# Six blocks' x and W1 products moved to the first steps of a graph layer kernel on one core

## The chip, the core and the metric

The kernel runs on one core of a Trainium2 chip. Its engines work side by side, each through its own list of instructions in program order: TensorE (PE in the profile; its weight loads are PEld), VectorE (DVE), ScalarE (ACT), GpSimd (POOL) and SyncE (SP), which here issues most DMAs. Matrix products land in PSUM banks, everything else lies in SBUF. The metric is the device time of one execution in microseconds (us); lower is better.

## The reference

One layer of a graph network with 12,500 nodes of 128 numbers and 412,500 edges of 48 numbers, sorted by destination:

```python
h   = relu(layernorm(x))                                  # 12500 x 128
agg = segment_sum(edge_attr_48, dst, num_segments=12500)  # 12500 x 48
u   = graph_globals[0]                                    # the same 64 numbers for every node
hid = relu(concat([h, agg, u]) @ W1 + b1)                 # 12500 x 256
out = x + hid @ W2 + b2                                   # 12500 x 128
```

All numbers are float32. Nearly all bytes that are read are the edges.

## The kernel before

**Edges.** They are taken in 58 steps (the last one smaller) of 8 chunks of 896 edges. A step's edges come in four loads (`load`, line 279) of 336 KB. VectorE compares destinations with a row of 0 to 31 (`onehot`, line 290); TensorE multiplies the one-hot matrices with the edges (`aggregate`, line 314) into a bank "ps"; ScalarE copies the bank to SBUF (`keep_sums`, line 335); VectorE makes a second one-hot matrix that places the chunks' windows (`place_columns`, line 352); two steps later TensorE multiplies with it (`place`, line 358) and VectorE adds the result to the running sums `aggT` (`add`, line 366). `aggT` lies as one column per node and has 112 rows; it is cleared in 16 parts of 797 columns, each part two steps before it is needed (`zero`, line 581).

**Nodes.** They are taken in 26 blocks: block 0 has 212 nodes (2 rows of 106), the others 512 (4 rows of 128), the last two 256 each. For a block, x is loaded (`load_x`), VectorE takes mean and variance (`stats`), ScalarE a root (`root`), VectorE makes scale and shift (`factors`), ScalarE normalises (`normal`, tile xn), TensorE transposes (`turn`, bank "pt"), ScalarE copies that to SBUF (`keep`, tile hT), TensorE multiplies with W1's rows for x (`first_h`, two halves, banks "ph") and later adds W1's rows for the sums (`first_a`) in the same bank, ScalarE adds the bias and cuts at zero (`relu`, tile hid), TensorE multiplies with W2 (`second`, bank "po"), VectorE adds x + b2 (`result`; GpSimd has made that sum in `plus_b2`), and GpSimd's queue stores it. A block's `first_a` can run only when the sums of all its nodes are there; its `first_h` needs only x.

**Banks.** "ph" has two buffers, "pt" and "po" have one each. A bank is written again only when whoever reads it is done.

**Order.** The schedule is written out by hand: the order in which the program issues instructions is the order of each engine. Each step s has two half-steps, 2s and 2s+1; `at(k, f, ...)` puts a function into half-step k, behind what was put there before. In a step come: `place` of two steps earlier, the work of half-step 2s, `add`, the work of half-step 2s+1, the step's `aggregate`, `keep_sums`, `place_columns`, and `onehot` of two steps later. The four loads of step s+3 stand between these. The pieces `turn`, `first_h`, `first_a`, `second` are put by a small planner (`piece`, line 643): each half-step has room for 1.25 us of such work (plus up to 0.5 left over, or what is lacking, from the half-step before), a piece goes to the first half-step from its due time on, and not before the piece put last, where the room is at least half its cost; costs are 0.16 r for `turn`, 0.22 r for each `first_h`, 0.27 r for `first_a`, 0.9 for each half of `second`, with r rows in the block. In steps with little such work, some pairs of edge products are put together as one of twice the width, which has fewer instructions and takes longer.

**Loads.** SyncE issues them in order. At most five counted loads are under way (`few`, line 272): each waits until the one five before it has landed. From step 1 on each also waits for the last TensorE instruction put in front of it.

**Other work near the start.** Destinations come in parts: part 0 (steps 0 to 3) and part 1 (16 steps) early. `shift_dst` and `own_and_ref` run on VectorE, `spread_dst` turns them on TensorE and copies on ScalarE, `middles` uses TensorE and then VectorE (part 0 in bank "po"). `check_dst` (line 261) is a check of the destinations on ScalarE, at half-steps 10 and 12 for parts 0 and 1. `bias_of_globals` (line 510) uses "po" as well. `spare` (line 593) is a product whose result is not used.

Of the kernel before, what the change touches and what calls it, by code (L numbers as in the profile page):

```python
# [8 lines left out]
F32 = mybir.dt.float32  # L9
# [13 lines left out]
def kernel(  # L23
# [75 lines left out]

    parts = [(0, 4 * CS)]  # L100
# [7 lines left out]
    aggT = const.tile([HI + DE, N + WG], F32)  # L108
# [32 lines left out]
    with fast:  # L141
# [224 lines left out]
        def add(s):  # L366
            _, v = nc.values_load_multi_w_load_instructions(
                at_i[0:1, s:s + 1], engines=[DVE], min_val=low(s), max_val=high(s),
                skip_runtime_bounds_check_because="clamped to these on the chip")
            to = aggT[:, ds(v[0], WG)]  # L370
            nc.vector.tensor_tensor(to, to, banks_p.pop(s)[:HI + DE, :WG], OP.add)  # L371

        def load_x(j):
            a, m, r = blocks[j]
            xt = xp.tile([P, 4, D], F32, name="xt")
            xv = xt.rearrange("p r d -> p (r d)")[:, :r * D]
            for p0, p1 in by_rows(m):
                now = nc.sync.dma_start(xv[p0:p1], rows_of(x, a + p0 * r, p1 - p0, r))
            if j > 1:
                few(now)  # L380
            xs[j] = xt
# [26 lines left out]
        def plus_b2(j):  # L408
            a, m, r = blocks[j]
            xb = mp.tile([P, 4, D], F32, name="xb", bufs=4)  # L410
            nc.gpsimd.tensor_tensor(xb[:m, :r], xs[j][:m, :r], b2_sb[:m, None, :].to_broadcast([m, r, D]), OP.add)  # L411
            xbs[j] = xb
# [9 lines left out]
        def turn(j):  # L422
            a, m, r = blocks[j]
            pt = ps_t.tile([P, 512], F32, name="pt")
            for q in range(r):
                transposed(pt[:, q * m:(q + 1) * m], ht[j][:m, q], ident[:m, :m])
            ht[j] = pt
# [20 lines left out]
        def first_h(j, h):  # L448
            n, small, ph = bank(j, h)
            product(ph, w1h[:, h * P:(h + 1) * P], ht[j][:, :n], start=(h == 0 or not small),  # L450
                             stop=False, skip_group_check=True)
            hids[j, h] = ph

        def first_a(j):
            a, m, r = blocks[j]
            n = m * r
            for q in range(0, n, 256):
                w = min(256, n - q)  # L460
                for h in range(NH):
                    c = BEFORE + a + q
                    k = slice(0, DE) if bank_is_shared(j) else slice(HI * h, HI * h + DE)
                    product(hids[j, h][:, q:q + w], w1a[k, h * P:(h + 1) * P], aggT[k, c:c + w],
                                     start=False, stop=True, skip_group_check=True)
# [92 lines left out]
        with tc.manual_schedule():  # L558
# [14 lines left out]
            ZN = 16  # L573
            zw = -(-aggT.shape[1] // ZN)

# [5 lines left out]
            def zero(i):  # L581
                nc.gpsimd.memset(aggT[:, i * zw:min((i + 1) * zw, aggT.shape[1])], 0.0)
# [72 lines left out]

            def behind(name, j):
                return where[name, j] // 2 * 2 + 2

            def turned(j):
                k = 8 + 3 * j if j < 2 else 2 * placed(ready[j]) - 2  # L660
                piece("turn", j, k, 0.16 * blocks[j][2], (turn, (j,)), (keep, (j,)))

            def hidden_x(j):
                us = 0.22 * blocks[j][2]
# [19 lines left out]
            for j in range(NBL):  # L684
                k = where["turn", j]
                if j > 1:
                    at(k - 17, load_x, j)
                near = j < 2
                at(k - (6 if near else 8), stats, j)
                at(k - (4 if near else 6), root, j)  # L690
# [6 lines left out]
            taken = {where["turn", j] for j in range(NBL)}  # L697
# [255 lines left out]
```

## Time and profile before

| | |
|---|---|
| median of 3 runs | 313.0 us (307.3 to 314.23) |
| the profiled execution | 310.81 us, its span 309.1 us |
| PE busy | 291.4 us (94%) |
| DVE busy | 231.8 us (75%) |
| ACT busy | 164.1 us (53%) |
| POOL busy | 78.5 us (25%) |
| moved by DMA | 95.15 MB, mean 308 GB/s |

The span runs from the first to the last instruction of the program; the profiled execution's own time is a little longer than its span. Busy time is the union of an engine's instructions, averaged over stages that differ, so the table alone does not say what sets the end.

### The profile page before, as it was taken

How to read it: one execution, taken by the hardware profiler on the slowest of the kernel's cores; microseconds unless marked ns; L12 is line 12 of the kernel's file. 1: busy time of each engine (PE TensorE's matmuls, PEld its weight loads, DVE VectorE, ACT ScalarE, POOL GpSimd, SP SyncE). 2: the span in 40 equal slices, each digit the busy share in tenths (PEclk: the TensorE clock that was granted, in tenths of full speed). 3: DMA queues.
4: the chain of work that ended last, by engine and by line, in shares of the span. 5: the costliest groups of instructions: out<-in, count | busy, mean ns of one | idle time of the engine just before them, and what ended most of it. 6: DMA issues, size and time to landing. Idle time of an engine off the chain costs nothing. (4 is left out here: it accounts for less than half of the span.)

```text
span 309.1 us, 14799 instructions
## 1 busy us (share of the span) xinstructions
PE 291.4 (94%) x6397; PEld 227.5 (74%) x6398; DVE 231.8 (75%) x530; ACT 164.1 (53%) x426; POOL 78.5 (25%) x87
## 2 busy tenths in 40 slices
PE   7888999999999999989999999999999899999982
PEld 3577767767877877866877887876887777786772
DVE  6867958987695967759976598779984899797221
ACT  2223696465564764645454487655452884665320
POOL 8221041032120544222134204123303033223000
PEclk9997999999999999999999999999999999999999
DMA  7999999999999999999999999999999999998102
GB/s 231 313 322 316 338 338 336 343 361 296 336 344 333 365 349 331 312 333 287 319 354 326 363 335 333 346 348 322 315 367 312 289 354 321 375 357 279 39 0 75
DMA packets 69717, 95.15 MB, mean 308 GB/s; under 512 B 5018, under 2 KB 64611, under 8 KB 69647
## 3 DMA queue, kind: packets, MB, share of 16 engines
q1 hardware_dynamic: 67439, 87.53, 85.3%
q0 software_dynamic: 2208, 6.63, 5.6%
q8 instruction: 51, 0.84, 1.1%
q14 instruction: 19, 0.16, 0.1%
HBM read 87.74 MB, written 6.40 MB: 305 GB/s over the span
## 5 line engine op out<-in xcount | busy, mean ns | idle before, releaser
L178 PE MATMUL ps<-e,oh 128*32 128x48 f32 (+1 forms) x5288 | 117.6, 218 | 7.2 <-issue 4.6
L178 PEld LDWEIGHTS ps<-e,oh 128*32 128x32 f32 (+1 forms) x5288 | 100.7, 116 | 31.4 <-issue 10.2
L294 DVE TENSOR_TENSOR oh<-iota,rel 128x1792 f32<-128x1792 f32 (+1 forms) x60 | 116.0, 1936 | 0.0
L340 ACT COPY sums<-ps 128x192 f32<-128x192 f32 (+1 forms) x165 | 43.1, 262 | 97.5 <-PE ps L178 94.9
L497 POOL DMA_DIRECT2D out_dram<-ot x25 | 14.0, 560 | 207.9 <-DVE ot L489 156.1
L371 DVE TENSOR_TENSOR aggT<-aggT,pp 112x246 f32 x58 | 23.7, 409 | 39.6 <-PE pp L178 30.3
L411 POOL TENSOR_TENSOR xb<-xt,b_sb 128x512 f32<-128x512 f32 (+2 forms) x26 | 46.5, 1792 | 15.3 <-DMA xt<-in_x_dram 9.8
L178 PE MATMUL po<-w,hid 128*128 128x128 f32 (+1 forms) x384 | 47.7, 276 | 1.3 <-ACTq L815 1.3
L178 PE MATMUL ph<-hT,w1h 128*128 128x512 f32 (+2 forms) x100 | 47.5, 578 | 0.6 <-ACT hT L432 0.6
L178 PEld LDWEIGHTS po<-w,hid 128*128 128x128 f32 (+1 forms) x384 | 44.9, 191 | 2.2 <-ACTq L815 1.4
L475 ACT ACTIVATE hid<-ph,bias 128x512 f32<-128x512 f32 (+2 forms) x49 | 30.4, 670 | 24.5 <-PE ph L178 23.3
L418 ACT ACTIVATE xn<-xt,sh,sc 128x128 f32<-128x128 f32 (+1 forms) x98 | 40.5, 483 | 0.5
L178 PE MATMUL pp<-place,sums 128*112 128x128 f32 x232 | 39.7, 295 | 0.0
L178 PEld LDWEIGHTS pp<-place,sums 128*112 128x112 f32 x232 | 29.2, 178 | 7.6 <-issue 1.5
L354 DVE TENSOR_TENSOR place<-iota,pos 128x256 f32<-128x256 f32 x58 | 34.3, 593 | 0.0
L178 PE MATMUL ph<-aggT,w1a 48*128 48x256 f32 (+1 forms) x192 | 28.3, 400 | 0.0
L432 ACT COPY hT<-pt 128x512 f32<-128x512 f32 (+2 forms) x26 | 26.7, 1026 | 3.1 <-PE pt L182 3.1
L489 DVE TENSOR_TENSOR ot<-po,xb 128x512 f32<-128x512 f32 (+2 forms) x25 | 16.6, 665 | 13.5 <-PE po L178 12.2
L178 PEld LDWEIGHTS ph<-aggT,w1a 48*128 48x128 f32 x192 | 17.3, 186 | 10.9 <-issue 7.8
L388 DVE BATCH_NORM_STATS2 st<-xt 128x6 f32<-128x128 f32 (+1 forms) x98 | 21.3, 279 | 1.8 <-DMA xt<-in_x_dram 1.8
L178 PEld LDWEIGHTS ph<-hT,w1h 128*128 128x128 f32 x100 | 16.2, 191 | 6.4 <-issue 3.3
L182 PE MATMUL pt<-ident,xn 128*128 128x128 f32 (+1 forms) x98 | 15.9, 282 | 0.0
(120 smaller groups left out, 139.7 us busy)
## 6 DMA issues: line engine op xcount, KB each, us to landing
e<-in_edge_attr_dram SPq DMA_DIRECT2D x230, 336.0 KB, 5.1
xt<-in_x_dram SPq DMA_DIRECT2D x23, 256.0 KB, 4.8
out_dram<-ot POOLq DMA_DIRECT2D x23, 256.0 KB, 5.5
di<-in_dst_dram SPq DMA_DIRECT2D x3, 448.0 KB, 6.9
xt<-in_x_dram SPq DMA_DIRECT2D x2, 128.0 KB, 4.2
out_dram<-ot SPq DMA_DIRECT2D x2, 128.0 KB, 2.6
di<-in_dst_dram SPq DMA_DIRECT2D x1, 154.0 KB
w1h<-in_L_gnn_W_dram POOLq DMA_DIRECT2D x1, 128.0 KB, 5.6
```

Source lines behind the costliest of these rows:

```text
L178: last[:] = [nc.tensor.matmul(*a, **k).ins.name]
L182: last[:] = [nc.tensor.transpose(*a, **k).ins.name]
L294: nc.vector.tensor_tensor(to, iota[:, None, :W].to_broadcast([P, n, W]), r[:, :, None].to_broadcast([P, n, W]), OP.is_equal)
L340: nc.scalar.copy(to[k, h], ps[k, h, None, o:o + DE].to_broadcast([k.stop - k.start, h.stop - h.start, 2, DE]))
L354: nc.vector.tensor_tensor(po, iota[:, None, :WP].to_broadcast([P, 2, WP]), pos[:, s, :, None].to_broadcast([P, 2, WP]), OP.is_equal)
L371: nc.vector.tensor_tensor(to, to, banks_p.pop(s)[:HI + DE, :WG], OP.add)
L388: nc.vector.bn_stats(st[:m, q, :], xs[j][:m, q, :])
L411: nc.gpsimd.tensor_tensor(xb[:m, :r], xs[j][:m, :r], b2_sb[:m, None, :].to_broadcast([m, r, D]), OP.add)
L418: nc.scalar.activation(xn[:m, q], xs[j][:m, q], AF.Relu, bias=shift[j][:m, q:q + 1], scale=scale[j][:m, q:q + 1])
L432: nc.scalar.copy(hT[:, :m * r].rearrange("d (p r) -> d r p", r=r), ht[j][:, :m * r].rearrange("d (r p) -> d r p", r=r))
L475: nc.scalar.activation(to, ph, AF.Relu, bias=bias[:, h:h + 1])
L489: nc.vector.tensor_tensor(ot[:m, :r], pos_o[j][:m, :r], xbs[j][:m, :r], OP.add)
```

## The change

Six blocks (`FIRST`, in the order 1, 2, 0, 3, 4, 5) get their x and their x W1 products early. x of these blocks and the products lie in columns of `aggT` that are cleared and used only later; `aggT` gets all 128 rows for this, while sums still use 112. The products are copied out of the bank on ScalarE (`keep_h`) and added back on VectorE (`add_h`) when the block's sums are there. The transposes of these blocks use bank "po". x of block 1 is loaded ahead of all edges, the others between the edge loads of steps 1 to 4; part 1 of the destinations is loaded between step 1's edge loads. All weights but W1's rows for x are loaded behind step 1's work. Two spare products go, and some of the early work on destinations moves by a half-step or a step.

```diff
+    FIRST = (1, 2, 0, 3, 4, 5)
+    ZN = 16
+    zw = -(-(N + WG) // ZN)
...
-    aggT = const.tile([HI + DE, N + WG], F32)
+    aggT = const.tile([P, N + WG], F32)
+    kept_x, kept_h = {}, {}
+    c0 = 4 * zw
+    for j in sorted(FIRST):
+        n = blocks[j][1] * blocks[j][2]
+        kept_x[j] = aggT[:, c0:c0 + blocks[j][2] * D].rearrange("p (r d) -> p r d", d=D)
+        c0 += blocks[j][2] * D
+        kept_h[j] = aggT[:, c0:c0 + NH * n].rearrange("p (h n) -> p h n", h=NH)
+        c0 += NH * n
...
-            xt = xp.tile([P, 4, D], F32, name="xt")
+            xt = kept_x[j] if j in FIRST else xp.tile([P, 4, D], F32, name="xt")
...
-            if j > 1:
+            if j != FIRST[0]:
                 few(now)
...
-            xb = mp.tile([P, 4, D], F32, name="xb", bufs=4)
+            xb = xs[j] if j in FIRST else mp.tile([P, 4, D], F32, name="xb", bufs=4)
...
-            pt = ps_t.tile([P, 512], F32, name="pt")
+            pt = ps_o.tile([P, 512], F32, name="po") if j in FIRST else ps_t.tile([P, 512], F32, name="pt")
...
-                             stop=False, skip_group_check=True)
+                             stop=j in FIRST, skip_group_check=True)
...
+        def keep_h(j, h):
+            if bank_is_shared(j):
+                n = blocks[j][1] * blocks[j][2]
+                nc.scalar.copy(kept_h[j], banks[j].rearrange("p (h n) -> p h n", h=NH)[:, :, :n])
+            else:
+                nc.scalar.copy(kept_h[j][:, h], hids[j, h])
+
+        def add_h(j):
+            if bank_is_shared(j):
+                n = blocks[j][1] * blocks[j][2]
+                to = banks[j].rearrange("p (h n) -> p h n", h=NH)[:, :, :n]
+                nc.vector.tensor_tensor(to, to, kept_h[j], OP.add)
+            else:
+                for h in range(NH):
+                    nc.vector.tensor_tensor(hids[j, h], hids[j, h], kept_h[j][:, h], OP.add)
...
         def load_weights():
             nc.gpsimd.dma_start(w1h, W1[0:D])
-            nc.gpsimd.dma_start(w1a[0:DE], W1[D:D + DE])
+
+        def load_weights_of_sums():
+            now = nc.gpsimd.dma_start(w1a[0:DE], W1[D:D + DE])
+            tc.add_manual_dep(now.ins, last[0], LANDED, reason="edges first")
...
+            load_x(FIRST[0])
             load_step(0)
+            load(1, 0)
+            load(1, 1)
             load_dst(1)
-            load_x(0)
-            load_step(1)
+            load(1, 2)
+            load(1, 3)
+            load_x(FIRST[1])
             load_step(2)
-            load_x(1)
+            load_x(FIRST[2])
+            load_x(FIRST[3])
             for s in range(3, AHEAD):
                 load_step(s)
+            load_x(FIRST[4])
...
+            for i, j in enumerate(FIRST):
+                r = blocks[j][2]
+                if i == len(FIRST) - 1:
+                    at(2, load_x, j)
+                at(2 * i, stats, j)
+                at(2 * i + 1, root, j)
+                at(2 * i + 1, factors, j)
+            for i, j in enumerate(FIRST):
+                at(2 * i + 2, normal, j)
+            for i, j in enumerate(FIRST):
+                r = blocks[j][2]
+                for k, us in ((2 * i + 3, 0.16 * r), (2 * i + 4, 0.44 * r)):
+                    room[k] = room.get(k, SHARE) - us
+                    work[k] = work.get(k, 0.0) + us
+                at(2 * i + 3, turn, j)
+                at(2 * i + 3, keep, j)
+                for h in range(NH):
+                    at(2 * i + 4, first_h, j, h)
+                    if h or not bank_is_shared(j):
+                        at(2 * i + 4, keep_h, j, h)
+                at(2 * i + 5, plus_b2, j)
...
-                piece("a", j, 2 * placed(ready[j]) + (4 if j == 0 else 2), 0.27 * r, (first_a, (j,)), (relu, (j,)))
+                piece("a", j, 2 * placed(ready[j]) + (4 if j == 0 else 2), 0.27 * r, (first_a, (j,)), *([(add_h, (j,))] if j in FIRST else []), (relu, (j,)))
...
-            at(0, shift_dst, 1)
-            at(2, spread_dst, 1, 0)
-            at(2, spread_dst, 1, 1)
+            at(2, shift_dst, 1)
+            at(4, spread_dst, 1, 0)
+            at(4, spread_dst, 1, 1)
             at(2, middles, 0)
-            at(4, own_and_ref, 1)
-            at(6, middles, 1)
+            at(3, load_weights_of_sums)
+            at(5, own_and_ref, 1)
+            at(7, middles, 1)
             at(10, check_dst, 0)
             at(12, check_dst, 1)
-            for k in (1, 3):
-                at(k, spare)
```

For the six blocks the planner places only `first_a` (with `add_h`) and `second`; their `turn`, `first_h` and the work around them stand at the half-steps written above, and `first_a` starts the bank anew.

More of the change, by code (lines that the diff above doesn't have):

```diff
@@ L107 @@
     relt = const.tile([P, T], F32)
-    aggT = const.tile([HI + DE, N + WG], F32)
+    aggT = const.tile([P, N + WG], F32)
[7 more added lines that the diff above has]
+        c0 += NH * n
+    assert c0 <= N + WG
     at_i = const.tile([1, NSP], I32)
@@ L369, in add @@
                 skip_runtime_bounds_check_because="clamped to these on the chip")
-            to = aggT[:, ds(v[0], WG)]
+            to = aggT[:HI + DE, ds(v[0], WG)]
             nc.vector.tensor_tensor(to, to, banks_p.pop(s)[:HI + DE, :WG], OP.add)
@@ L458, in first_a @@
             n = m * r
+            if j in FIRST:
+                for h in range(NH):
+                    _, small, hids[j, h] = bank(j, h)
             for q in range(0, n, 256):
@@ L461, in first_a @@
                 for h in range(NH):
+                    begin = j in FIRST and q == 0 and (h == 0 or not small)
                     c = BEFORE + a + q
@@ L464, in first_a @@
                     product(hids[j, h][:, q:q + w], w1a[k, h * P:(h + 1) * P], aggT[k, c:c + w],
-                                     start=False, stop=True, skip_group_check=True)
+                                     start=begin, stop=True, skip_group_check=True)
         def relu(j):
@@ L572 @@
                            allow_small_or_imprecise_dtypes=True)
-            ZN = 16
-            zw = -(-aggT.shape[1] // ZN)
             def clear_tail():
@@ L581, in zero @@
             def zero(i):
-                nc.gpsimd.memset(aggT[:, i * zw:min((i + 1) * zw, aggT.shape[1])], 0.0)
+                nc.gpsimd.memset(aggT[:HI + DE, i * zw:min((i + 1) * zw, aggT.shape[1])], 0.0)
             zero(0)
@@ L653 @@
             piece.last = 0
+            for i, j in enumerate(FIRST):
[14 more added lines that the diff above has]
+                at(2 * i + 3, keep, j)
+                for h in range(NH):
+                    at(2 * i + 4, first_h, j, h)
+                    if h or not bank_is_shared(j):
+                        at(2 * i + 4, keep_h, j, h)
+                at(2 * i + 5, plus_b2, j)
             def behind(name, j):
@@ L659, in turned @@
             def turned(j):
-                k = 8 + 3 * j if j < 2 else 2 * placed(ready[j]) - 2
+                if j in FIRST:
+                    return
+                k = 2 * placed(ready[j]) - 2
                 piece("turn", j, k, 0.16 * blocks[j][2], (turn, (j,)), (keep, (j,)))
             def hidden_x(j):
+                if j in FIRST:
+                    return
                 us = 0.22 * blocks[j][2]
@@ L684 @@
             for j in range(NBL):
+                if j in FIRST:
+                    continue
                 k = where["turn", j]
[L686 to L690, printed above, removed]
+                at(k - 17, load_x, j)
+                at(k - 8, stats, j)
+                at(k - 6, root, j)
                 at(k - 4, factors, j)
@@ L694 @@
             at(where["a", 0] - 2, bias_of_globals)
-            taken = {where["turn", j] for j in range(NBL)}
+            taken = {where["turn", j] for j in range(NBL) if j not in FIRST}
             def apart(k, f, *a):
```

## The prediction

> **What bounds the kernel now.** I read the page's slices first, then the windows, then the timelines of TensorE (PE), ScalarE (ACT), VectorE (DVE) and SyncE (SP) over the first 100 us, where the change lies.
>
> ```profile
> DMA  7999999999999999999999999999999999998102
> ...
> 20.00:40.00 20.00, 17.10 (x333) 14.54 (x332) 16.46 (x51) 10.11 (x30) 3.24 (x3) 0.91 1.00 330
> 40.00:60.00 20.00, 20.00 (x455) 15.29 (x456) 15.51 (x35) 14.56 (x38) 5.70 (x6) 1.00 1.02 338
> ...
> 290.00:300.00 10.00, 10.00 (x225) 8.29 (x224) 2.31 (x6) 2.71 (x7) 0.00 (x0) 1.00 0.06 23
> ```
>
> The first row gives the DMA engines' busy share in 40 slices, the others PE, PEld, DVE, ACT and POOL (each with its count), then PE's clock, the DMA share and GB/s. Two resources are full at once: the DMA engines from the second slice until the edges are in, and PE from 40 us to the end, where it works on alone (DMA 0.06). Both limits have to be followed.
>
> ```profile
> 17.00 1.37 PE L178 MATMUL ps<-e,oh 128*64 128x96 f32 x26 [0.54 <-DMA e<-in_edge_attr_dram]
> ...
> 25.72 2.50 PE L178 MATMUL ps<-e,oh 128*64 128x96 f32 x26 [0.58 <-DMA e<-in_edge_attr_dram]
> ...
> 39.89 1.98 PE L178 MATMUL ph<-hT,w1h 128*128 128x512 f32 x4 [0.61 <-ACT hT L432]
> ...
> 159.70 2.49 PE L178 MATMUL ps<-e,oh 128*32 128x48 f32 x84
> ```
>
> The columns are start, duration, engine, line, operation, tiles, count and the wait before it. In steps 1 to 5 PE waits for edges (the first two rows); from then on the loads run a little ahead and PE is late by its own work, in program order. The third row is the one I weigh most: the product of x and W1 of block 1 waits 0.61 us for ScalarE's copy hT, because ScalarE, also in order, had to finish something else first. The last row (step 30) took 2.49 us where an equal group takes 2.11 (45.80 below): a short wait of about 0.4 us, the only place after step 5 where I find the loads still setting the pace. So time that PE loses before step 30 is time lost at the end, but for 0.4 us; time that PE gains before step 30 is given back to the loads there.
>
> **The change, part by part.** It moves, for six blocks, the turning of x and the products with W1 from steps 4 to 15 into steps 1 to 7, adds a copy out of the sums' bank on ScalarE (keep_h) and an addition on VectorE (add_h), and removes two spare products. PE's prices are start-to-start differences of these rows.
>
> ```profile
> 45.80 2.11 PE L178 MATMUL ps<-e,oh 128*32 128x48 f32 x84
> 47.83 0.69 PE L178 MATMUL pp<-place,sums 128*112 128x128 f32 x4
> 48.36 1.95 PE L178 MATMUL po<-w,hid 128*128 128x128 f32 x16
> 50.15 1.02 PE L178 MATMUL ph<-hT,w1h 128*128 128x512 f32 x2
> 51.10 1.87 PE L178 MATMUL ps<-e,oh 128*32 128x48 f32 x96
> 52.90 0.69 PE L178 MATMUL pp<-place,sums 128*112 128x128 f32 x4
> ...
> 54.38 1.14 PE L178 MATMUL ph<-aggT,w1a 48*128 48x256 f32 x8
> 55.45 0.66 PE L182 MATMUL pt<-ident,xn 128*128 128x128 f32 x4
> 56.03 1.87 PE L178 MATMUL ps<-e,oh 128*32 128x48 f32 x96
> ...
> 92.51 0.69 PE L178 MATMUL pp<-place,sums 128*112 128x128 f32 x4
> ```
>
> A step's edges: 2.03 us (84 records) to 1.80 (96). Placing: 0.53. Second layer of a block: 1.79. One product of x and W1: 0.95, so 1.9 for both halves. Product of the sums: 1.07. Turning: 0.58. Step 7 ends at 47.83 and step 16 at 92.51.
>
> ```profile
> 12.23 0.73 PE L182 MATMUL pt<-ident,df 128*128 128x128 f32 x4 [1.37 <-DVE df L198]
> ...
> 13.26 0.38 PE L178 MATMUL po<-own,same_c 32*128 32x8 f32 x2
> ...
> 13.92 1.13 PE L178 MATMUL ph<-iota,ones 128*128 128x512 f32 x2
> ...
> 29.14 0.36 PE L182 MATMUL pt<-ident,xn 106*128 106x106 f32 x2
> 29.43 0.60 PE L178 MATMUL po<-u,w1u 64*128 64x1 f32 x4
> ...
> 33.44 0.88 PE L178 MATMUL ph<-hT,w1h 128*128 128x212 f32 x4
> 34.25 0.98 PE L178 MATMUL ph<-aggT,w1a 48*128 48x212 f32 x4
> ...
> 35.75 2.03 PE L178 MATMUL ps<-e,oh 128*32 128x48 f32 x88
> ```
>
> Turning destinations: 1.03; middles: 0.66; a spare pair: 1.13. The small block 0: turning 0.29, products with W1 0.81, with the sums 0.9. Bias: 0.6.
>
> ```profile
> 35.93 0.93 ACT L258 ACTIVATE sc<-df 32x896 f32<-32x896 f32 x1
> ...
> 38.79 1.05 ACT L432 COPY hT<-pt 128x512 f32<-128x512 f32 x1
> 39.63 0.87 ACT L340 COPY sums<-ps 128x192 f32<-128x192 f32 x3
> 40.53 1.65 ACT L418 ACTIVATE xn<-xt,sh,sc 128x128 f32<-128x128 f32 x4
> 42.08 0.94 ACT L258 ACTIVATE sc<-df 128x896 f32<-128x896 f32 x1
> ...
> 44.98 0.28 ACT L397 ACTIVATE sc<-mv,eps 128x4 f32<-128x4 f32 x1
> ...
> 13.00 0.60 ACT L252 COPY rel<-pt 128x512 f32<-128x512 f32 x1 [1.26 <-PE pt L182]
> ```
>
> On ScalarE hT costs 1.05, keeping the sums 0.87, normalising 1.55, a root 0.3. check_dst(0), from 35.93 to 38.79, costs 2.86 and check_dst(1), from 42.08 to 44.98, costs 2.90: these are what hT stood behind in the row above. keep_h is not in this trace; a copy of the same size out of a bank took 0.60 (13.00) and hT, which also reorders, 1.05. I take 0.55, nearest to the plain copy; with 1.05 each a block would pay 1.0 more on ScalarE.
>
> *Step 1.* Its turning of block 1 writes the bank "po" (one buffer), which middles(0) used just before; VectorE reads that bank only after it has done, in order, the statistics of block 2 and shift_dst.
>
> ```profile
> 11.21 0.15 DVE L196 CAST first<-di 128x1 f32<-128x1 int32 x1 [1.14 <-DMA di<-in_dst_dram]
> ...
> 12.00 2.02 DVE L294 TENSOR_TENSOR oh<-iota,rel 128x1792 f32<-128x1792 f32 x1
> ...
> 21.27 0.87 DVE L388 BATCH_NORM_STATS2 st<-xt 128x6 f32<-128x128 f32 x4 [0.24 <-DMA xt<-in_x_dram]
> ...
> 22.34 0.53 DVE L354 TENSOR_TENSOR place<-iota,pos 128x256 f32<-128x256 f32 x1
> ```
>
> Block 2's x is loaded behind step 1's last edges, which landed at 17.00; the new order puts block 1's x ahead of them and the small loads of weights behind, so I leave 17.0 for it. Statistics 1.07 and shift 0.79 give 18.9, some short reads 19.3, turning 19.9, edges 22.0. Before, step 1 ended at 18.4: 3.6 late. The spare products that filled this wait are gone.
>
> *Steps 2 and 3.* 0.53 + 1.9 + 1.03 + 0.58 + 1.9 = 5.9 and 0.53 + 1.9 + 0.29 + 0.66 + 1.9 = 5.3. End 33.2.
>
> *Step 4.* Turning waits for xn, ready 0.87 + 1.55 = 2.4 into the step; bias_of_globals uses po too and waits for hT (root 0.3, then 1.05) until 4.4. Then 0.6 + 2.03: 7.0 us, 2.5 of them waits.
>
> *Step 5.* 0.53 + 1.9 + 0.58 + 0.9 + 1.8 = 5.7, with 0.3 of waits 6.0. But ScalarE does sums 0.87, xn 1.55, two keep_h 1.1, check_dst(0) 2.86, root 0.3, hT 1.05, so hT of block 4 is ready 7.8 into the step.
>
> *Step 6.* PE starts at 6.0 of that clock, and block 4's products wait from 6.5 to 7.8. ScalarE then does block 0's relu (0.7), sums and xn, until 10.9: turning of block 5 ends at 11.5. Then keep_h twice and check_dst(1), 4.0, and hT, 1.05: 15.9. The second layer of block 0 stands next on PE, needs po, and waits for that copy: 4.4 us. With 0.9 for it and 1.7 for the edges the step ends at 18.5, that is 12.5 us long.
>
> *Step 7.* 0.53 + 1.9 + 0.6 of wait for a bank + 1.07 + 1.75 = 5.9.
>
> Sum: 22.0 + 5.9 + 5.3 + 7.0 + 6.0 + 12.5 + 5.9 = 64.6 against 47.8: 16.8 late. (The planner's room at even half-steps is 1.25 - 1.76, below zero there, which is what puts block 0's second layer at half-step 13, next to that turning.)
>
> *Steps 8 to 16* have lost the moved work: nine times 0.53 + 2.03, four products of sums 4.3, four second layers 7.2, one turning, 0.9 of destinations: 36.1 against 92.5 - 47.8 = 44.7. That gives 8.6 back, and 8.2 remain. From step 17 the plan is the old one by its totals.
>
> *Loads.* They are issued three steps ahead, tied to PE's pace.
>
> ```profile
> 43.23 0.34 SPq L378 DMA_DIRECT2D xt<-in_x_dram  x1
> ```
>
> This load (block 5, issued in step 5) could have gone when PE had done step 5's small work (35.75), and went 7.5 us later, being held by the loads before it. So a PE up to 7.5 us late stops no load; one 16.8 late stops them for about 9.3 us, which DMA engines at 1.00 can't make up. The two limits give nearly the same loss, 8.2 and 9.3.
>
> ```profile
> 26.00:29.00 3.00, 3.00 (x30) 2.78 (x29) 2.22 (x15) 0.70 (x3) 1.27 (x1) 0.50 0.88 276
> ```
>
> *Clock.* Behind the short waits of step 3 PE was granted 0.50, and the group at 25.72 took 2.50 instead of 1.37, 1.1 more. The changed kernel has two longer holes (some 6 us in step 1, 4.4 in step 6): 2.2 us. The Trainium skill, "TensorE: Matmul & The Clock Gate", in "Why this matters for your kernels", says that a hole of about 3 us takes the clock to half; here a clock of 0.50 followed waits of which the longest was 0.58, so the trace is less forgiving than the page. By its window of about 3.4 us at half speed the two holes would cost an estimated 3.4.
>
> *Hidden.* add_h goes to VectorE, 15.51 of 20 us busy:
>
> ```profile
> L489 DVE TENSOR_TENSOR ot<-po,xb 128x512 f32<-128x512 f32 (+2 forms) x25 | 16.6, 665 | 13.5 <-PE po L178 12.2
> ```
>
> An addition from a bank costs 0.67, so 1.3 a block, about what the moved statistics free; uncovered on PE, five and a half blocks would be 7 us. The weights that POOL now issues behind step 1's work are first needed in step 4, after 33 us, and would cost only what they landed later than that; the moved x loads keep SP's order and bytes, apart from blocks 4 and 5 coming some steps earlier; the additions of b2 run on POOL, wanted only by the results.
>
> **Sum:** 8.2 to 9.3, plus 2.2 for the clock, less 0.4 at step 30: +10 to +11.1. The profiled execution took 310.8 (span 309.1 and 1.7 around it), 2.2 below the median of 313.0. I forecast 310.8 + 10.7 = 321.5.
>
> **Rivals.** (1) *No change that shows*: if ScalarE's copies don't hold PE (hT ready in time, po free), steps 4 to 7 lose 2.5 + 0.3 + 7.0 + 0.6 = 10.4 less; 6.4 late at step 7 is less than the 8.6 given back and less than the 7.5 that stops loads. Then the loads decide at step 30: 310.4, and with half the waits about 314. For it: DMA at 1.00 throughout. Against: the wait at 39.89. (2) *Faster*: the early holes of PE (2.9 us in 20:40, 1.1 of slow clock, 2.3 of spare products) are filled and the loads turn out able to go faster with PE ahead: 310.8 - 6.3 = 304.5. Against: a DMA share of 1.00 leaves no such speed. (3) *Heavier*: keep_h costs 1.05, which adds 1.0 on ScalarE in front of hT in each of steps 2 to 6: 321.5 + 5 = 326.5, and to 330 if the loads, stopped as much longer, are then the limit. For it: ScalarE is the engine that holds PE; against: the plain copy's 0.60.
>
> **How the numbers follow.** Forecast (316 to 326) 0.62; no change 0.20; faster 0.08; heavier 0.10. Leaving out the faster case and the far end of the heavier one gives 310 to 328. Over 2% is about 6.3 us, roughly what a measurement of this kernel tells from no change: slower 0.68, same 0.24, faster 0.08.
>
> **What would show it.** On PE a second-layer product po<-w,hid of block 0 in step 6 that waits some 4 us for ACT hT; first products of block 4 that wait for hT; a turning in step 1 that waits for DVE; a DMA share below 0.9 somewhere between 40 and 65 us; step 7 ending near 65. It is wrong if ScalarE is idle there, if the DMA share stays at 1.00, or if PE catches up before step 30 by more than 8.6 us.

## The result and the profile after

The changed kernel takes 327.38 us in the median (327.18 to 330.79), against 310.83 us for the kernel before on the same chip: a ratio of 1.0618, 95% interval 1.0495 to 1.0740. Executions of one kernel differ by a few per cent, and all ratios here compare the faster ones alone, so they aren't the quotients of the medians. The changed kernel's profiled execution took 327.18 us with a span of 325.4, against 310.81 and 309.1: 16.3 us more.

The slices of the page of the changed kernel, in the order PE, clock, DMA:

```profile
PE   7489695699999999999899999999999999999992
...
PEclk9969989599999999999999999999999999999998
DMA  7999965289999999999999999999999999999302
```

Where DMA had a row of nines there is now a hole in slices 6 to 8 (40 to 65 us); PE has holes in slices 2, 5, 7 and 8, and its clock dips three times. The page gives 95.15 MB for both kernels: nothing more is moved, but for a while less per us. The same in windows of 10 us (columns as in the prediction: PE, PEld, DVE, ACT, POOL, clock, DMA share, GB/s):

```profile
40.00:50.00 10.00, 9.67 (x209) 7.54 (x209) 3.91 (x12) 6.13 (x17) 1.26 (x1) 0.84 0.71 216
50.00:60.00 10.00, 3.97 (x12) 1.80 (x12) 5.71 (x8) 9.17 (x24) 0.00 (x0) 0.84 0.39 116
60.00:70.00 10.00, 9.95 (x237) 7.25 (x237) 2.94 (x6) 3.32 (x8) 3.05 (x4) 0.81 0.57 161
70.00:80.00 10.00, 10.00 (x218) 9.00 (x218) 8.53 (x10) 3.46 (x11) 0.60 (x1) 1.00 0.89 276
80.00:90.00 10.00, 9.55 (x256) 8.22 (x258) 8.35 (x18) 2.85 (x8) 1.33 (x2) 1.00 1.01 338
```

From 40 to 80 us the DMA engines lose (0.29 + 0.61 + 0.43 + 0.11) x 10 = 14.4 us of their time; after that they are full again and can't win it back. That is nearly the whole loss of 16.3; TensorE's own lateness, further down, is as large. Between 50 and 60 ScalarE is busy for 9.17 us and TensorE for 3.97.

Who stops the loads stands in SyncE's waits of the changed kernel between 35 and 75 us (what it waited for: us in total, times, longest):

```profile
SPq L142 <- PE po L193: 9.1, 2, 7.7
SPq L142 <- PE ps L193: 6.7, 4, 3.0
SPq L142 <- PE po L197: 5.1, 3, 3.1
...
SPq L142 <- DMA e<-in_edge_attr_dram: 2.4, 5, 0.5
```

The edge loads wait for TensorE, to whose pace they are tied, and hardly for earlier loads. TensorE's own timeline in the changed kernel shows what it waited for:

```profile
17.88 1.08 PE L197 MATMUL po<-ident,xn 128*128 128x128 f32 x4 [6.30 <-DVE dev L254]
18.90 3.79 PE L193 MATMUL ps<-e,oh 128*32 128x48 f32 x84
...
39.45 0.70 PE L193 MATMUL po<-u,w1u 64*128 64x1 f32 x4 [2.74 <-ACT hT L447]
40.09 3.54 PE L193 MATMUL ps<-e,oh 128*32 128x48 f32 x84
...
51.31 1.98 PE L193 MATMUL ph<-hT,w1h 128*128 128x512 f32 x4 [1.21 <-ACT hT L447]
...
59.42 2.04 PE L193 MATMUL po<-w,hid 128*106 128x128 f32 x8 [4.62 <-ACT hT L447]
61.40 2.64 PE L193 MATMUL ps<-e,oh 128*32 128x48 f32 x108
...
69.75 0.69 PE L193 MATMUL pp<-place,sums 128*112 128x128 f32 x4
```

Three long waits: the turning in step 1 for VectorE (6.30), the bias in step 4 (2.74) and block 0's second layer in step 6 (4.62), both for ScalarE's hT. Behind each, the edge products are slow: 3.79 and 3.54 us for the 84 records that took 2.11 at 45.80 in the kernel before, and 2.64 for 108 records that took 1.63 in the version with bank "pt" below. Step 7 ends at 69.8 instead of 47.8, 22.0 late.

ScalarE in step 6, on its own timeline of the changed kernel, is what the prediction described:

```profile
54.45 1.07 ACT L475 COPY aggT<-ph 128x512 f32<-128x512 f32 x2
55.41 0.96 ACT L273 ACTIVATE sc<-df 128x896 f32<-128x896 f32 x1
...
58.34 1.03 ACT L447 COPY hT<-po 128x512 f32<-128x512 f32 x1
```

Two copies keep_h (0.53 each), then the check of the destinations from 55.41 to 58.34, and only then the hT for which "po" and so the second layer wait.

### The profile page after: what moved, and what is told of

Same layout as the page of the kernel before. It is cut to its first block, busy times and chain, and to the rows that moved or that the text cites. A ratio compares the mean times of both kernels' runs of the same rounds, so it can differ in the third digit from the quotient of the medians.

```text
span 325.4 us, 14757 instructions
## 1 busy us (share of the span) xinstructions
PE 296.6 (91%) x6373; PEld 232.0 (71%) x6374; DVE 238.6 (73%) x541; ACT 169.4 (52%) x437; POOL 75.8 (23%) x87
## 2 busy tenths in 40 slices
DMA packets 69717, 95.15 MB, mean 292 GB/s; under 512 B 5018, under 2 KB 64611, under 8 KB 69647
## 5 line engine op out<-in xcount | busy, mean ns | idle before, releaser
L193 PE MATMUL ps<-e,oh 128*32 128x48 f32 (+1 forms) x5268 | 121.5, 222 | 4.5 <-issue 2.2
L193 PEld LDWEIGHTS ps<-e,oh 128*32 128x32 f32 (+1 forms) x5268 | 104.5, 119 | 27.8 <-issue 7.1
L193 PE MATMUL po<-w,hid 128*128 128x128 f32 (+1 forms) x384 | 48.7, 280 | 6.2 <-ACT hT L447 4.6
L426 POOL TENSOR_TENSOR xb<-xt,b_sb 128x512 f32<-128x512 f32 (+1 forms) x20 | 36.0, 1801 | 0.2
L369 DVE TENSOR_TENSOR place<-iota,pos 128x256 f32<-128x256 f32 x58 | 32.7, 564 | 0.0
L433 ACT ACTIVATE xn<-xt,sh,sc 128x128 f32<-128x128 f32 x76 | 31.4, 484 | 0.9 <-DVE sh L420 0.5
L525 DVE TENSOR_TENSOR ot<-po,xb 128x512 f32<-128x512 f32 (+1 forms) x19 | 12.8, 673 | 13.4 <-PE po L193 12.1
L447 ACT COPY hT<-pt 128x512 f32<-128x512 f32 (+1 forms) x20 | 20.7, 1037 | 2.1 <-PE pt L197 1.9
L403 DVE BATCH_NORM_STATS2 st<-xt 128x6 f32<-128x128 f32 x76 | 16.5, 278 | 0.0
L412 ACT ACTIVATE sc<-mv,eps 128x4 f32<-128x4 f32 (+2 forms) x26 | 7.6, 293 | 10.1 <-DVE mv L405 7.1
```

The source lines that it names most:

```text
L193: last[:] = [nc.tensor.matmul(*a, **k).ins.name]
L369: nc.vector.tensor_tensor(po, iota[:, None, :WP].to_broadcast([P, 2, WP]), pos[:, s, :, None].to_broadcast([P, 2, WP]), OP.is_equal)
L403: nc.vector.bn_stats(st[:m, q, :], xs[j][:m, q, :])
L433: nc.scalar.activation(xn[:m, q], xs[j][:m, q], AF.Relu, bias=shift[j][:m, q:q + 1], scale=scale[j][:m, q:q + 1])
L447: nc.scalar.copy(hT[:, :m * r].rearrange("d (p r) -> d r p", r=r), ht[j][:, :m * r].rearrange("d (r p) -> d r p", r=r))
L525: nc.vector.tensor_tensor(ot[:m, :r], pos_o[j][:m, :r], xbs[j][:m, :r], OP.add)
```

## The experiments

The theories were these. **A**: TensorE's holes in steps 1 to 7, made by the order around bank "po", by the checks on ScalarE and by VectorE's order, with the slow clock behind them, make TensorE late; what goes beyond 7.5 us stops loads, and that time is lost. **B**: the new order of the loads costs by itself. **C**: the added copies and additions cost by themselves. All ratios are to the kernel before, run beside it on the same chip. "Late" is the end of step 7's edge products against 47.8 in the kernel before (there the start of the row behind it, so that lateness is stated up to 0.1 us too large).

### One part of the order undone at a time

*Bank.* The six early blocks are turned in bank "pt" as the others:

```diff
-            pt = ps_o.tile([P, 512], F32, name="po") if j in FIRST else ps_t.tile([P, 512], F32, name="pt")
+            pt = ps_t.tile([P, 512], F32, name="pt")
```

> The early blocks are turned in bank pt, as before the change, and no longer in po; nothing else differs. My theory (A): PE's holes of 6.3, 2.7 and 4.6 us stand where po is held by VectorE or by ScalarE's copy, PE falls 22 us behind by step 7, and whatever exceeds some 7.5 us stops the loads for good. Then the three holes shrink (the first to about 2.5, the second goes, the third moves to the next product and leaves 1.3), step 7 ends near 59 instead of 69.8, and the time is about 315. Rival (B): it is the x loads ahead of the edges, or the bytes' order, that costs: 325 to 328, with step 7 a little earlier and the same hole in the DMA. Rival (C): ScalarE's and VectorE's added copies and additions cost the time: 324 to 327.

Measured: 316.75 us, ratio 1.0191 (1.0127 to 1.0255). The waits of 6.30, 2.74 and 4.62 are gone; the longest that remain are 1.99 us and less; step 7 ends at 60.1. The profiled execution is the shortest of the four (313.57 us).

*Checks.* The two checks of destinations leave the first steps:

```diff
-            at(10, check_dst, 0)
-            at(12, check_dst, 1)
+            at(20, check_dst, 0)
+            at(24, check_dst, 1)
```

> The two checks of destinations go from half-steps 10 and 12 to 20 and 24; nothing else differs. A: ScalarE's queue of steps 5 and 6 loses 2.9 us each, the wait of block 4's products (1.2) goes, the wait for po in step 6 falls from 4.6 to about 1.7, the half-speed stretch behind it too; 5 to 6 us less: about 321.5. B: no change, 327. C: no change beyond 1 us, since the added copies stay.

Measured: 319.16 us, ratio 1.0243 (1.0186 to 1.0301). Step 7 ends at 64.3, and in step 6 one wait is left on TensorE's timeline:

```profile
54.27 1.12 PE L193 MATMUL po<-w,hid 128*106 128x128 f32 x8 [1.73 <-ACT hT L447]
55.33 2.72 PE L193 MATMUL ps<-e,oh 128*32 128x48 f32 x108
```

4.62 us became 1.73, and the product itself took 1.12 instead of 2.04. The clock fell a little later all the same: the edges behind it took 2.72 us, as slow as the 2.64 in the changed kernel, at a granted clock of 0.50 from 56 to 58 us. So the slow stretch, which was expected to go, stayed; the time is lower than the expected 321.5 us nevertheless.

*VectorE.* `shift_dst(1)` and `middles(0)` go ahead of the statistics in step 1:

```diff
+            at(2, shift_dst, 1)
+            at(2, middles, 0)
             for i, j in enumerate(FIRST):
...
-            at(2, shift_dst, 1)
...
-            at(2, middles, 0)
```

> In step 1 shift_dst(1) and middles(0) go ahead of the second block's statistics on VectorE; nothing else differs. A: VectorE reads the bank po about 14 us into the span instead of 17.8, the hole of 6.3 us in step 1 becomes about 3, and if PE keeps its clock, the edges behind it take 2.1 instead of 3.8: 3 to 5 us less, 322.5 to 324.5. B and C: no change, 327.

Measured: 326.25 us, ratio 1.0460 (1.0337 to 1.0582). TensorE's timeline in step 1:

```profile
14.89 1.09 PE L197 MATMUL po<-ident,xn 128*128 128x128 f32 x4 [3.45 <-DVE dev L254]
15.91 3.79 PE L193 MATMUL ps<-e,oh 128*32 128x48 f32 x84
```

The hole is half as long, but the edges behind it still take 3.79: halving a hole that the clock notices anyway saves only the hole's half. Step 7 ends at 66.8. The median lies above the 322.5 to 324.5 of theory A, near the 327 of no change, and the interval overlaps that of the change, so only the trace (3.0 us less late) shows the gain.

*Clock.* Eleven spare products fill the three holes, and nothing else is changed:

```diff
             at(2, middles, 0)
+            for _ in range(5):
+                at(2, spare)
...
                 at(2 * i + 5, plus_b2, j)
+                for _ in range((0, 0, 0, 2, 0, 4)[i]):
+                    at(2 * i + 3, spare)
```

> Eleven spare products, whose results aren't used, fill PE's three holes (5 in step 1, 2 in step 4, 4 in step 6); the holes' ends stay. It tells what the half clock behind the holes costs by itself. A: the edges behind the holes take 2.1, 2.1 and 1.7 instead of 3.8, 3.5 and 2.6, and block 0's second layer 1.0 instead of 2.0; 5 us of PE, which come off the stop of the loads: 322. If the half clock costs nothing at the end, 327.

Measured: 320.77 us, ratio 1.0321 (1.0221 to 1.0422), span 319.6 at a mean clock of 0.994. In step 1 a wait is left behind the spare products, and the edges there stay slow, against the expected 2.1 (TensorE's timeline of this kernel):

```profile
17.94 0.63 PE L197 MATMUL po<-ident,xn 128*128 128x128 f32 x4 [1.94 <-DVE dev L254]
18.50 3.58 PE L193 MATMUL ps<-e,oh 128*32 128x48 f32 x84
```

Windows over step 4's edges and step 6's end, first this kernel, then the changed one:

```profile
40.00:44.00 4.00, 3.95 (x38) 2.47 (x34) 2.92 (x10) 2.83 (x8) 0.35 (x1) 1.00 1.02 338
58.00:62.00 4.00, 4.00 (x109) 2.58 (x105) 0.84 (x2) 1.37 (x4) 3.05 (x4) 1.00 0.64 163
```

```profile
40.00:44.00 4.00, 4.00 (x89) 3.75 (x90) 3.49 (x11) 0.32 (x1) 0.00 (x0) 0.60 0.68 223
58.00:62.00 4.00, 2.58 (x40) 2.32 (x44) 0.42 (x1) 1.35 (x3) 0.00 (x0) 0.50 0.00 0
```

In these two steps the clock is 1.00 where it was 0.60 and 0.50, although the work that TensorE waited for came at most 0.5 us sooner. Step 7 ends 4.4 us earlier, at 65.4, and the span is 325.4 - 319.6 = 5.8 us shorter: that is what filling the holes is worth here, with two of the three slow stretches gone.

*All three orders* (bank, checks, VectorE) at once:

> The changed kernel with three of its orders altered at once: the early blocks turned in bank pt, the two checks of destinations at half-steps 20 and 24, and the shift of destinations and the middles put ahead of the statistics of step 1. Theory A (TensorE's holes in steps 1 to 7 and the slow clock behind them, which stop the loads beyond 7.5 us): the holes of step 1 and step 6 nearly gone, step 7 ends at 53 to 57 instead of 69.8, the loads are hardly stopped, and the time is 309 to 314 us. It isn't much below the kernel before, because the loads run at a DMA share of 1.00 and still set the pace at step 30. Theory B (the order of the loads costs): 320 us or more. Theory C (the added copies and additions cost by themselves): 318 us or more.

Measured: 313.51 us, ratio 1.0113 (1.0024 to 1.0202). Step 7 ends at 53.4, 5.6 late, and the loads are hardly stopped; the windows of this kernel show a DMA share of 0.94 and more:

```profile
50.00:60.00 10.00, 9.95 (x273) 8.17 (x277) 7.07 (x9) 3.38 (x9) 0.60 (x1) 1.00 1.00 321
60.00:70.00 10.00, 10.00 (x260) 8.82 (x247) 9.00 (x14) 7.10 (x19) 1.32 (x2) 1.00 0.94 304
```

So about five of the six per cent come from the order of the work around the moved parts, and not from the moving. And with the orders repaired the change is still not faster than the kernel before. One slow stretch is left, in step 1: behind a wait of 2.15 us the edges still take 3.79. What this execution loses at the end came late: at step 52 TensorE is 0.2 us ahead of the kernel before, and from 270 us on it stops for 3.3 us in three places where nothing in the profile releases it.

### The other two theories

*Copies and additions left out:*

```diff
-                    if h or not bank_is_shared(j):
-                        at(2 * i + 4, keep_h, j, h)
...
-... (first_a, (j,)), *([(add_h, (j,))] if j in FIRST else []), (relu, (j,)))
+... (first_a, (j,)), (relu, (j,)))
```

> The changed kernel without the copies out of the bank on ScalarE and without the additions on VectorE; the hidden layer of the six early blocks then lacks the part of x. Theory A: ScalarE has 1.1 us less a block, the wait of 4.62 us for hT in step 6 falls by about that, and the time falls to 322 to 326 us. Theory C (copies and additions are the cause): 315 us or less. Theory B: 326 us or more.

Measured: 324.56 us, ratio 1.0460 (1.0387 to 1.0532). The wait in step 6 is 3.65 us instead of 4.62, as A says. C falls as the main cause: in step 6 the copies matter as 1 us more on an engine that already holds TensorE.

*Only the new order of the loads*, the products made where the kernel before makes them. The first version:

```diff
+    EARLY_J = ()
...
-            for i, j in enumerate(FIRST):
...
-                at(2 * i + 5, plus_b2, j)
+            at(2, load_x, FIRST[-1])
...
-                k = 2 * placed(ready[j]) - 2
+                k = 8 + 3 * j if j < 2 else 2 * placed(ready[j]) - 2
```

> Only the new order of the loads: x of six blocks, the destinations and the weights are loaded as in the changed kernel, but the turning and the products of x and W1 are made when the kernel before made them, with no copies out of the bank and no additions. Theory A: the loads' order costs next to nothing, 309 to 314 us. Theory B (the order of the loads, x in front of edges and weights behind step 1, is the cause): most of the loss is here, 322 us or more. Theory C says as A.

Measured: 317.76 us, ratio 1.0244 (1.0184 to 1.0303), between the two answers. The edit had brought a hole of its own, seen on VectorE's and TensorE's timelines of this kernel:

```profile
21.93 0.49 DVE L404 BATCH_NORM_STATS2 st<-aggT 106x6 f32<-106x128 f32 x2 [9.86 <-DMA aggT<-in_x_dram]
```

```profile
27.15 1.17 PE L194 MATMUL pp<-place,sums 128*112 128x128 f32 x4 [11.73 <-DVE place L370]
```

Block 0's x is loaded third in the new order, while its statistics stood in step 1 as before, with all of step 1's one-hot work behind them. The run says nothing on B. Repeated with these statistics in step 3, and with the work on destinations and the two spare products back where the kernel before has them (the main lines of the edit):

```diff
-                at(k - (6 if near else 8), stats, j)
-                at(k - (4 if near else 6), root, j)
-                at(k - 4, factors, j)
+                late = 2 * (j == 0)
+                at(k - (6 if near else 8) + 2 * late, stats, j)
+                at(k - (4 if near else 6) + late, root, j)
+                at(k - 4 + late, factors, j)
...
-            at(2, shift_dst, 1)
+            at(0, shift_dst, 1)
...
+            for k in (1, 3):
+                at(k, spare)
```

> The new order of the loads alone, without the hole that the run with this order before had (there VectorE waited 9.86 us for block 0's x in step 1): the statistics of block 0 now stand in step 3, behind the landing of its x, and the work on destinations is where the kernel before has it. The turning and the products of x and W1 are made when the kernel before made them. Theory A (holes of TensorE): no hole, so 309 to 313 us. Theory B (the order of the loads by itself): 316 us or more, as the run with the hole (317.8).

Measured: 312.59 us against 311.95, ratio 1.0024 (0.9969 to 1.0078). B falls: the order of the loads costs nothing that can be measured, at most 0.8% by the interval.

*Three early blocks instead of six*, and then the same with bank "pt" and VectorE's order repaired:

```diff
-    FIRST = (1, 2, 0, 3, 4, 5)
+    FIRST = (1, 2, 0)
...
-            load_x(FIRST[3])
...
-            load_x(FIRST[4])
...
-                if i == len(FIRST) - 1:
-                    at(2, load_x, j)
```

> Only the first three blocks (1, 2, 0) get their x and products early; blocks 3, 4 and 5 are treated as in the kernel before. Theory A: the hole of step 1 stays (about 6 us), those of steps 5 and 6 for block 4 and block 0's second layer go, step 7 ends at 54 to 57, at most 1 or 2 us of loads are stopped, and the time is 310 to 315 us. A loss in proportion to the number of blocks (theory C, or B) gives half the loss, about 319 us.

> Only blocks 1, 2 and 0 early, turned in bank pt, and the shift of destinations and the middles ahead of the statistics in step 1. Theory A: the wait of about 6 us in step 1 falls to 3 us or less, step 7 ends at 50 to 53, and the time is 309 to 312 us: as fast as the kernel before and no faster, since the loads are held at a share of 1.00. If the loss of the version with three blocks has another cause than holes, it stays at 312.6 us.

Measured: 312.63 us, ratio 1.0101 (1.0009 to 1.0193), and 311.50 us, ratio 1.0079 (1.0035 to 1.0123). With three blocks the hole of step 1 stays (5.95 us) and step 7 ends 8.5 late; little is lost. Half the blocks cost a sixth of the loss, which no price per block explains; lateness does, 8.5 us instead of 22.0, of which all but 1.0 lies within the 7.5. Repaired, step 7 ends 4.8 late. No version that I ran is faster than the kernel before.

### What the move could bring at most, and what lateness costs

*Less work.* In the kernel before, the products of x and W1 of blocks 0 to 5 are simply not made:

```diff
             n, small, ph = bank(j, h)
+            hids[j, h] = ph
+            if j < 6:
+                return
...
```

> The kernel before without the products of x and W1 of blocks 0 to 5 (their hidden layer lacks the part of x): TensorE has 5 x 1.9 + 0.8 = 10.3 us less to do between steps 4 and 16, with nothing added anywhere. It is the most that moving these products away could bring. If the loads set the pace as well (theory A: DMA share of 1.00, and waits for edges at step 30), the time is 308 to 311 us, at most 2 us less than before. If TensorE alone sets the end, it is 300 to 302 us.

Measured: 310.79 us against 311.95, ratio 1.0008 (0.9956 to 1.0059). TensorE's waits over the whole span, first of this kernel, then of the kernel before:

```profile
PE ps L178 <- DMA e<-in_edge_attr_dram: 10.4, 19, 1.2
PE ps L178 <- issue: 2.7, 5, 1.7
```

```profile
PE ps L178 <- issue: 4.6, 9, 1.0
PE ps L178 <- DMA e<-in_edge_attr_dram: 2.5, 5, 0.6
```

Ten us less of work, and eight us more of waiting for edges, 19 times instead of 5. Even a move of these products that cost nothing would gain nothing that this measurement could show, since the edges come no sooner.

*Lateness by itself.* Twenty spare products ahead of step 7's edges, with nothing of the change, and 14 blocks' products of x and W1 left out so that TensorE can catch up:

```diff
-            if j < 6:
+            if j < 14:
...
             for k in (1, 3):
                 at(k, spare)
+            for _ in range(20):
+                at(15, spare)
```

> The kernel before with one artificial delay of TensorE and none of the change: 20 spare products (20 x 0.95 = 19 us) ahead of the edge products of step 7, and the products of x and W1 of blocks 0 to 13 left out (their hidden layer lacks the part of x), so that TensorE has about 21 us less to do between step 7 and step 34 and could catch up. Some 17 us late at step 7, against the kernel before. If only TensorE's work sets the end, it has caught up by step 34 and the time is 309 to 313 us. If loads that are stopped while TensorE is more than 7.5 us late are lost for good (theory A), the DMA share falls between 45 and 70 us, the loads run 17 - 7.5 = 9.5 us later from then on, and the time is 318 to 322 us.

Measured: 318.78 us against 310.44, ratio 1.0285 (1.0238 to 1.0333). The windows of this kernel, and TensorE's waits between 72 and 210 us:

```profile
60.00:70.00 10.00, 10.00 (x95) 4.89 (x95) 0.00 (x0) 0.00 (x0) 0.00 (x0) 1.00 0.04 8
70.00:80.00 10.00, 10.00 (x258) 8.72 (x254) 7.89 (x13) 6.58 (x17) 1.88 (x2) 1.00 0.91 288
```

```profile
PE ps L178 <- issue: 6.4, 7, 1.6
PE ps L178 <- DMA e<-in_edge_attr_dram: 3.8, 4, 1.8
```

In the first window TensorE is busy throughout at a clock of 1.00, and the loads stand still (0.04): it is lateness that stops them, whatever its cause. Later TensorE has caught up so far that it waits for edges again, up to 1.8 us at a time; the time is lost nevertheless. The sizes agree only roughly: the profiled execution, at 325.44 us the longest of six (the others 318.1 to 319.0), was 22.7 late at step 7 and not 17, so what the 7.5 us give for the other executions isn't shown. For the profiled one they give 15.2, and its span was 14.6 beyond 309.1.

### Lateness and loss side by side

From TensorE's timelines and the spans (profiled executions, us):

| version | step 7 late | less 7.5 | step 16 late | span beyond 309.1 |
|---|---|---|---|---|
| the change | 22.0 | 14.5 | 15.4 | 16.3 |
| VectorE's order | 19.0 | 11.5 | 13.1 | 13.7 |
| holes filled | 17.6 | 10.1 | 10.4 | 10.5 |
| checks later | 16.5 | 9.0 | 10.5 | 8.5 |
| bank "pt" | 12.3 | 4.8 | 5.0 | 2.7 |
| three blocks | 8.5 | 1.0 | 5.8 | 2.4 |
| all orders | 5.6 | none | 1.8 early | 2.5 |
| three blocks, orders | 4.8 | none | 2.3 | 1.1 |

Eight versions with different causes of lateness lie within about 2.5 us of the line "less 7.5". Each row is one execution, and the spans of the kernel before alone range from 305.2 to 315.7, so the line is no sharper than that. The version without copies was profiled in its longest execution (328.34 us, median 324.56) and lies off the line: 19.8 late, 17.4 lost.

The table doesn't tell what passes the lateness on to the end, for there is a second account. TensorE is full, and what it can give back after step 7 is the work that was moved away from steps 8 to 16: 5.8 to 7.3 us in the versions with six blocks, about as much as the 7.5 of the loads. The column for step 16 fits the versions that are late there within 3.4 us. In the changed kernel TensorE waits for no edges between steps 1 and 16, and from 100 us to the end only twice (time in total, times, longest):

```profile
PE ps L193 <- DMA e<-in_edge_attr_dram: 1.5, 2, 0.9
```

So there the stopped loads and TensorE's own work cost nearly the same, and the loads add at most the 1.5 us of these two waits. That the loads are a limit by themselves is shown by the two runs above (less work, lateness by itself), where TensorE had less to do and waited for edges. That TensorE is one is shown by the run with the hole of 11.73 us: 8.6 late at step 7, with no work taken from steps 8 to 16, it is 8.6 late at step 16 as well and loses 7.4, far more than the 1.1 beyond the slack.

## Why the prediction was right in direction and too low in size

The forecast was slower, 321.5 us in a range of 310 to 328; the median was 327.38, inside the range, near its end. On the profiled execution I forecast 10.7 us more and 16.3 were measured. By its steps:

- **What bounds the kernel**: right. Two limits at once; for gains the loads decide, as the run with less work shows more strongly than I had put it: no more came of it than my 0.4 us of room at step 30, of which the trace shows 0.2 as a wait of the weight loads for edges.
- **Step 1**: right in cause (the turning waits for VectorE behind the statistics), 22.7 for 22.0 in its end. The turning began at 17.88 and not at 19.3, since block 2's x came earlier; the slow clock, which I had priced apart at 1.1 and which cost 2.1, took that back.
- **Steps 2, 3, 5, 7**: 6.2, 4.9, 5.9 and 5.8 us for 5.9, 5.3, 6.0 and 5.9. The prices taken from the trace of before carried over.
- **Step 4**: wrong, 9.8 us for 7.0. I had ScalarE go from the root to hT without a wait. Its timeline in the changed kernel shows the root waiting for VectorE:

```profile
38.16 0.30 ACT L412 ACTIVATE sc<-mv,eps 128x4 f32<-128x4 f32 x1 [1.29 <-DVE mv L405]
```

  So hT came late and TensorE waited 2.74 us in one piece; behind that the clock fell, which cost 3.54 - 2.11 = 1.4 more.
- **Step 6**: right in cause and order; the wait for "po" was 4.62 for 4.4, the wait of block 4's products 1.21 for 1.3. The step took 14.6 us for 12.5, the difference nearly all the clock: 2.04 instead of 1.12 for the second layer, 2.64 instead of some 1.8 for the edges.
- **Clock**: the step that failed; the term was mis-sized. I had two slow stretches of 1.1 us, 2.2 in all, and no charge for the waits of 2.5 us that I forecast in step 4, although my own row had shown a clock of 0.50 behind waits of at most 0.58. There were three stretches, of about 2.1 (edges 1.7, turning 0.4), 1.4 and 1.8 us, 5.3 in all, in steps 1, 4 and 6, so they all count into the lateness. Without them step 7 was 22.0 - 5.3 = 16.7 late, where I had 16.8; that this fits so well is partly luck, since step 1 came 1.4 us sooner and step 4's wait 1.3 longer than I had them. By the loads' account my terms give 16.8 + 2.2 - 7.5 = 11.5, the measured lateness 22.0 - 7.5 = 14.5, and the DMA share lost 14.4.
- **Loads and TensorE**: that the two limits give nearly the same loss came out, at 14.5 and 15.4 instead of 9.3 and 8.2. The slack of 7.5 us fits the versions within 2.5. What steps 8 to 16 give back was mis-sized as well: 6.5 us where I had 8.6, and not because the loads held TensorE, which waited for no edges there. From step 16 to the end only 0.9 us were added, although TensorE waited 1.5 us for edges there.
- **Hidden**: right. keep_h took 0.53 for an assumed 0.55, add_h 0.65; the weights behind step 1 and the moved loads cost nothing that the run with that order alone could measure.
- **Rivals**: *heavier* gave the right number (326 to 330) by the wrong mechanism: a keep_h of 1.05 isn't there. *No change* is what the three repaired orders make of it (1.0113). *Faster* is ruled out by the run with less work, as far as 0.4% (its interval begins at 0.9956).
- **What would show it**: four of the signs came (4.62 us for hT before block 0's second layer, block 4's products waiting, the turning waiting for DVE, DMA below 0.9 between 40 and 65 us); step 7 ended at 69.8 and not near 65, and that is the miss.

## What to carry to other kernels

Where transfers run at a share of 1.00 and are issued in the pace of a compute engine, lateness of that engine is forgiven only as far as both allow it: the slack of the transfers (7.5 us here) and the work that the engine has less of later (6.5 us here). What goes beyond either is lost, so add up every cause of lateness, the clock's too, before anything is subtracted. Before work is moved off a full engine, leave it out altogether in one run: here that showed in a single number that the move had nothing to gain. And look at what an in-order engine has queued in front of the copy that frees a bank: two checks behind which TensorE waited 0.61 us in the kernel before cost some 8 us here (327.38 against 319.16 with the checks later) once a bank waited behind them.

## What was unexpected of the hardware

The clock falls sooner and costs more than I had priced: a single wait of 2.74 us was followed by this window of the changed kernel,

```profile
40.00:42.00 2.00, 2.00 (x65) 1.87 (x67) 1.80 (x3) 0.00 (x0) 0.00 (x0) 0.50 1.01 321
```

and each slow stretch cost 1.4 to 2.1 us. In the version with three blocks a wait of 1.87 us between busy stretches was enough; the second layer behind it took twice its 1.95 us, at a clock of 0.50 from 51 to 54 us:

```profile
50.45 3.83 PE L193 MATMUL po<-w,hid 128*128 128x128 f32 x16 [1.87 <-ACT hid L511]
```

A single wait of 1.57 us in the version with bank "pt" was followed by a clock of 1.00. The Trainium skill, "TensorE: Matmul & The Clock Gate", in "HAM oscillation — how this bites in real kernels", gives as the rule no idle gaps above some 3.4 us; by it step 4 would have stayed at full clock. The measurement decides: 0.50 behind 2.74 us, and behind 1.87.

TensorE also stops now and then in the middle of a group of edge products with nothing in the profile to release it ("issue" in its waits): 4.6 us in 9 such stops in the kernel before, 6.4 in 7 in the run with the artificial delay, up to 1.7 us each. They fall in other steps in each version. What they are stays open; they are of the size of the differences of 1% between the last versions (3.3 us at the end of the version with all orders), and those aren't explained further here.
